# A gated-scan and Hadamard FFN layer: an earlier load of x, a norm's ScalarE work spread over two units, and transposes evicted by VectorE alone

## The chip, the cores and the metric

The kernel runs on one core of a Trainium2 chip. The metric is the device time of one execution in microseconds (us); with one core there is no slowest core to look for. The engines are called as in the profile: PE is TensorE (PEld its weight loads), ACT is ScalarE, DVE is VectorE, POOL is GpSimd, SP is SyncE, which here only issues DMAs.

## What is computed

Four sequences (B = 4) of T = 512 tokens with D = 512 features pass through one layer, all in float32. Cut to what matters:

```python
def attn(h):                                   # Wi, Wf, Wg, Wo: 512 x 512
    i, f, g = h @ Wi.T, h @ Wf.T, h @ Wg.T
    gate = sigmoid(f)
    v = silu(i) * (1.0 - gate)
    o = scan over tokens of  o_t = gate_t * o_(t-1) + v_t
    o = o * rsqrt(mean(o * o) + 1e-5) * gnorm_w * silu(g)
    return o @ Wo.T

def ffn(h):                                    # W1, W3: 2048 x 512, W2: 512 x 2048
    hidden = silu(h @ W1.T) * (h @ W3.T)
    return fwht(hidden) @ W2.T                 # Walsh-Hadamard transform over 2048

x = x + layernorm(attn(layernorm(x)))
x = x + layernorm(ffn(layernorm(x)))
```

## The kernel before, in words

**Products.** Every large product is done by a Strassen-Winograd scheme: seven products of quarter blocks instead of eight. `seven` (L387) makes the seven steps in the order P1, P2, P6, P5, P7, P3, P4 (`ORDER`, L31). P1, P6, P7 and P4 add up in one PSUM bank, called X; P5 and P3 in a bank Z; P2 has a bank Y. Each step is eight matmuls into its bank, and then the bank as it stands goes to a quarter of the result in SBUF: ACT copies it at P1, P6, P5 and P4 (L413), DVE adds it to what lies there at P2, P7 and P3 (L411). (Where the result is itself added to an older one, all seven are DVE additions.) Since P6 goes on adding into the bank of P1, it must wait until that bank was copied; in the same way P3 waits for the copy of P5, and P4 for the addition of P7.

**Units.** One call of `project` is a unit: two projections of 512 tokens by 128 or 256 features. A sequence has three attention units (`attn_unit`, L450) and eight FFN units m = 0 to 7 (`ffn_unit`, L533). In an FFN unit the result d_f is followed by ACT's Silu (L535), DVE's product ht (L441) and four DVE sums over blocks of ht (L122 to L125). Every two FFN units, `ffn_out` (L549) multiplies their ht with the transformed W2 (X_po, Y_po, Z_po at L559); the transform of W2 itself runs between the products as `transform_high` and `transform_low` (h and g).

**Order.** PE and SP run in the order in which the program calls them. Between two products of a unit, `run` (L99) calls `slot`, which takes the next waiting piece of other work from the list `fill` (down projections, transposes, W2's transform): after each product where the unit is dense, else after products 1, 3, 5 and 6. ACT, DVE and POOL are ordered by the framework's scheduler, by priorities (`high_priority`) and by `behind(what)` (L207), which lets a block be issued only after the instruction last noted under that name in `read`: "P7" is the latest DVE addition of a P7, "copy" the latest ACT copy of a bank.

**x and the norms.** x of a sequence is loaded by `load_x` (L112) as four tiles of 256 KB. `normalize_tiles` (L236) makes a layernorm of two of its four 128-token tiles: statistics and their root on DVE and POOL (L252, L253, L218, L221, L229), then one ACT instruction per tile that writes xn (L262). For the first sequences (`ON_TENSOR`, L234) PE transposes xn (`transposes`, L327): in two halves h = 0 and 1, each with one 128x256 piece of four PSUM banks, of which ACT copies two (L348) and DVE two (L350); after the second half DVE forms four sums of blocks (L129 to L132), which the products P6, P5, P7 and P4 read. For all other norms ACT writes xn in a permuted order, POOL issues its write to DRAM (xnd, L270), and `load_fold` (L358) reads it back through SP as fold, which DVE transposes in 32x32 blocks (L378) and sums up.

**The places concerned.** In FFN unit 3 of sequence 0, x of sequence 2 is loaded (L757). Ahead of FFN unit 4 of sequences 0 and 1 the attention norm of sequences 2 and 3 is made (L759), in one piece; in unit 6 its fold is loaded (L761), and in unit 7 it is transposed (L763).

Of the kernel before, what the change touches and what calls it, by code (L numbers as in the profile page):

```python
# [42 lines left out]
def kernel(  # L43
# [14 lines left out]
    nc = tc.nc  # L58
    B, T, D = x.shape
# [25 lines left out]
    def bank(name):  # L85
        return psum.tile([P, 2, H], F32, tag="ps", name=name)
# [4 lines left out]
    fill = deque()  # L91

    def slot():
        if fill:
            make = fill.popleft()
            if make is not None:
                make()

    def run(products, dense):  # L99
        for k, make in enumerate(products):  # L100
            make()
            if dense or k in (1, 3, 5, 6):
                slot()

# [7 lines left out]
    def load_x(b):  # L112
        xs[b] = xpool.tile([P, NT, D], F32, tag="x", name=f"x_{b}")
        for i in range(NT):
            eng = nc.scalar if b == 0 else nc.sync
            eng.dma_start(out=xs[b][:, i, :], in_=x[b, ts(i, P), :])
# [10 lines left out]
    def combine_right(t, eng):  # L127

        eng.tensor_sub(t[:, T1], t[:, B12], t[:, B11])  # L129
        eng.tensor_sub(t[:, T2], t[:, B22], t[:, T1])  # L130
        eng.tensor_sub(t[:, T3], t[:, B22], t[:, B12])
        eng.tensor_sub(t[:, T4], t[:, B21], t[:, T2])  # L132
# [33 lines left out]
    def combine_weights(n=None):  # L166
        for _ in range(len(uncombined) if n is None else n):
            key, t = uncombined.pop(0)
            combine_left(t, nc.vector)
            kept(key, t)  # L170
# [9 lines left out]
    def load_ffn_w(b, m):  # L180
        ffn_w[b, m] = weight(w1, "w1", m, b), weight(w3, "w3", m, b)
# [25 lines left out]
    def behind(what):  # L207


        return tc.issue_after(read[what].ins)  # L210
# [13 lines left out]
    def scales(mv, eps, name):  # L224

        n = mv.shape[1]
        r = inverse_root(mv, eps, name)
        nb = small.tile([P, n], F32, tag="nb", name=f"nb_{name}", bufs=4)
        i = nc.vector.scalar_tensor_tensor(nb, mv[:, :, 0], -1.0, r, ALU.mult, ALU.mult)  # L229
        return r, nb, i  # L230

    xns, xnd = {}, {}
# [3 lines left out]
    def normalize_tiles(b, name, i0, n, later=False):  # L236

        if (name, b) not in xns:
            xns[name, b] = work.tile(
                [P, NT, D], F32, tag="wide", name=f"xn_{name}_{b}", bufs=3
            )
        t = xns[name, b]
        st = small.tile([P, n, 6], F32, tag=f"st{n}", name=f"st_{name}_{b}_{i0}")
        mv = small.tile([P, n, 2], F32, tag=f"mv{n}", name=f"mv_{name}_{b}_{i0}")  # L250
        for k in range(n):
            nc.vector.bn_stats(st[:, k, :], xs[b][:, i0 + k, :])  # L252
            nc.vector.bn_aggr(mv[:, k, :], st[:, k, :])  # L253
        r, nb, read["nb"] = scales(mv, EPS, f"{name}_{b}_{i0}")

        def apply():
            for k in range(n):
                x_t, to = xs[b][:, i0 + k, :], t[:, i0 + k, :]
                if (name, b) not in ON_TENSOR:
                    x_t = x_t.rearrange("p (i a c) -> p i c a", c=ND, a=32)  # L260
                    to = to.rearrange("p (i c a) -> p i c a", c=ND, a=32)
                read["xn"] = nc.scalar.activation(  # L262
                    to, x_t, AF.Identity, bias=nb[:, k : k + 1], scale=r[:, k : k + 1]
                )
            if (name, b) not in ON_TENSOR:
                if (name, b) not in xnd:
                    xnd[name, b] = scratch.tile(
                        [NT, P, D], F32, tag=f"xn_{name}_{b}", name=f"xnd_{name}_{b}"
                    )
                nc.gpsimd.dma_start(  # L270
                    out=xnd[name, b][i0 : i0 + n].rearrange("t p d -> p t d"),
                    in_=t[:, i0 : i0 + n, :],
                )

        if later:
            return apply
        apply()

    def normalize(b, name, n=2):
        for i in range(0, NT, n):  # L280
            normalize_tiles(b, name, i, n)
# [45 lines left out]
    def transposes(b, name):  # L327

        xn = xns.pop((name, b))
        xt = work.tile([P, 7, 2, H], F32, tag="xt", name=f"xt_{name}_{b}", bufs=2)
        xts[name, b] = xt
        pt = []

        def make(h):
            if h == 0:
                pt.extend(bank(f"pt_{name}_{b}_{c}") for c in range(ND))  # L340
            for i in range(2 * h, 2 * h + 2):
                for c in range(ND):
                    nc.tensor.transpose(pt[c][:, h, ts(i % 2, P)], xn[:, i, c::ND], ident)
            with tc.high_priority(offset=URGENT):
                for c in range(ND):
                    to = xt[:, (B11, B12)[h] if c < 2 else (B21, B22)[h], c % 2, :]
                    if c % 2:
                        nc.scalar.copy(to, pt[c][:, h, :])  # L348
                    else:
                        read["xt"] = nc.vector.tensor_copy(to, pt[c][:, h, :])  # L350
                if h:
                    combine_right(xt, nc.vector)

        return [partial(make, h) for h in range(2)]
# [190 lines left out]
    def load_down_w(b, part):  # L545
        for m in range(part * NS, (part + 1) * NS):
            down_w[b, m] = again(("w2", m), b, stream2)
# [108 lines left out]
    def transform_low(m):  # L656

        def make(k):  # L660
            w = low_w[m]
            if k == 0 and m + 2 < NU:
                load_low(m + 2)
            blocks = ((B11, B12), (B21, B22))[k]
            t = w[:, blocks[0] : blocks[1] + 1 : blocks[1] - blocks[0]]
            p = bank(f"g_{m}_{k}")
            nc.tensor.matmul(p, h16_sb, t, start=True, stop=True)
            nc.scalar.mul(t, p, 1.0 / FF**0.5)
            if k == 1:
                combine_right(w, nc.vector)  # L670
                kept(("w2", m), w)

        return [partial(make, k) for k in range(2)]
# [33 lines left out]
    with behind("P3"):  # L707
        with tc.high_priority(offset=URGENT):
            combine_weights(2)
        with tc.high_priority(offset=SOON):  # L710
            apply = [normalize_tiles(1, "a", i, 2, True) for i in (0, 2)]
# [6 lines left out]
        with behind("P2"):  # L718
            prepare_wo(wo_t[0])

    def norm_behind_copy():
        with behind("copy"):
            for make in apply:
                make()

    fill.extend([wo_behind_sum, norm_behind_copy] + transposes(1, "a"))
    attn_unit(0, 2)
    load_attn_w(1, 1)
    fill.extend([None] * 3 + attn_out(0))
# [11 lines left out]
    for b in range(B):  # L741
        last = b == B - 1
        for m in range(NU):
            if m + 1 < NU:
                load_ffn_w(b, m + 1)
            if b == 0 and m % NS == 0:
                for k in range(m + 2, min(m + 2 + NS, NU)):
                    fill.extend(transform_low(k))
            if m == 0 and not last:
                fill.extend([None] * 4 * (b > 0) + attn_out(b + 1))  # L750
            if m and m % NS == 0:
                if last and m == NU - NS:
                    fill.extend([None] * 8)
                fill.extend([None] + ffn_out(b, m // NS - 1))
            if m % NS == 1:
                load_down_w(b, m // NS)
            if m == 3 and b == 0:  # L757
                load_x(2)
            if m == 4 and b + 2 < B:  # L759
                normalize(b + 2, "a")  # L760
            if m == 6 and not last:  # L761
                load_fold(*((b + 2, "a") if b + 2 < B else (b + 1, "f")))
            if m == NU - 1 and not last:  # L763
                transpose_fold(*((b + 2, "a") if b + 2 < B else (b + 1, "f")))
            ffn_unit(b, m, b == 0)
            with behind("P7"):
                combine_weights()
        tail = ffn_out(b, NU // NS - 1)
        if b + 2 < B:
            load_attn_w(b + 2, 0)  # L770
            load_fold(b + 1, "f")
            fill.extend([None] + tail)
            for u in range(3):
                if u < 2:
                    load_attn_w(b + 2, u + 1)
                else:
                    load_ffn_w(b + 1, 0)
                if u == 1:
                    transpose_fold(b + 1, "f")
                attn_unit(b + 2, u)  # L780
            if b + 3 < B:
                load_x(b + 3)
        elif not last:
            load_ffn_w(b + 1, 0)
            fill.extend([None] + tail)
        else:
            fill.extend(tail)
            flush()
# [34 lines left out]
```

## Time and profile before

| what | value |
|---|---|
| median of 3 runs | 840.94 us (840.87 to 841.08) |
| the profiled execution | 841.11 us |
| its span from first to last instruction | 839.3 us |
| mean granted PE clock | 0.993 |
| x of sequence 2: issued, landed | 195.44 to 197.7, 206.4 to 208.6 us |
| xn of sequence 2 on ACT (4 tiles) | 211.98 to 217.3 us |
| xn of sequence 3 on ACT (4 tiles) | 394.34 to 401.9 us |
| ACT instruction for one permuted tile of xn, mean | 1.28 to 1.35 us |
| ACT copy of one bank (128x512) | 0.58 us |
| DVE addition of one bank (128x512) | 0.69 us |
| PE, eight 128x256 matmuls of one product, start to start | 1.73 us |

The profile's page lists the busy time of each engine, the chain of work that ended last, groups of instructions by source line with the wait in front of them, and DMA transfers. A timeline gives each engine's instructions in order of time, with the number of equal instructions that were merged, and in brackets how long the engine stood before, and what ended that. A name such as X_f is the PSUM bank X of an FFN unit; X_a is one of an attention unit, X_po one of a down projection. "out<-in" are the tiles written and read. Only what stands in PE's way, or slows its clock, can be seen in the span directly.

### The profile page before, as it was taken

The page shows a single profiled execution, that of the slowest core. Times are in us where ns is not written, and L with a number is a line of the kernel's source. Part 1 is how long each engine was busy: PE and PEld are TensorE (multiplying, and loading weights), DVE is VectorE, ACT ScalarE, POOL GpSimd, SP SyncE. Part 2 cuts the span into 40 slices and gives each one's busy share as a digit, 9 for nine tenths or more (in the row PEclk, how much of TensorE's full clock was granted, in tenths as well). Part 3 has the DMA queues.
Part 4 walks back from the last instruction along what each step waited for, and adds up shares of the span by engine and source line. Part 5 has one row for each costly group of instructions (what it writes and reads, how often), then busy time and mean ns, then how long its engine had stood idle before and what let it go on. Part 6 is the DMA issues. An engine that isn't in the chain of part 4 may idle for free.

```text
span 839.3 us, 9824 instructions
## 1 busy us (share of the span) xinstructions
PE 817.5 (97%) x3728; PEld 703.8 (84%) x3728; DVE 457.6 (55%) x920; ACT 269.1 (32%) x386; POOL 68.9 (8%) x112
## 2 busy tenths in 40 slices
PE   7999999999799999999999999999999999999995
PEld 4788888888688888888888888888888888888884
DVE  6386796754656557537435545737336434534445
ACT  4554462532311225227312123524321121322111
POOL 5120101210200001003000000102000000100000
PEclk9999999999899999999999999999999999999998
DMA  9995369596968625826563622835353642625101
GB/s 335 414 409 211 110 230 348 210 343 239 330 209 263 231 88 184 355 89 254 182 197 156 202 88 95 330 152 197 117 214 90 273 174 89 226 94 214 70 19 50
DMA packets 65743, 169.54 MB, mean 202 GB/s; under 512 B 4768, under 2 KB 40224, under 8 KB 65696
## 3 DMA queue, kind: packets, MB, share of 16 engines
q1 hardware_dynamic: 56528, 125.65, 42.3%
q0 software_dynamic: 8448, 41.96, 12.7%
q10 hardware_dynamic: 720, 1.31, 0.4%
q8 instruction: 29, 0.48, 0.2%
q14 instruction: 18, 0.15, 0.0%
HBM read 125.90 MB, written 42.99 MB: 201 GB/s over the span
## 4 chain that ended last, share of the span: by engine, by line
PE 84%; DVE 5%; DMA 5%; ACT 2%; issue 2%; SPq 1%; POOL 1%; POOLq 0%; DVEq 0%; ACTq 0%
PE X_f L426 23%; PE X_po L559 12%; PE Z_f L426 12%; PE X_a L426 8%; PE Z_po L559 6%; PE Y_f L426 6%; PE Z_a L426 5%; PE Y_po L559 3%; PE X_y L512 3%; DMA w2p<-in_W_dram 3%; PE Y_a L426 2%; PE Z_y L512 2%; DMA x<-in_x_dram 2%; DVE x L316 1%; PE Y_y L512 1%
## 5 line engine op out<-in xcount | busy, mean ns | idle before, releaser
L426 PE MATMUL X_f<-xt_f,w 128*128 128x256 f32 x1024 | 241.5, 379 | 0.9 <-ACT d_f L413 0.9
L426 PEld LDWEIGHTS X_f<-xt_f,w 128*128 128x128 f32 x1024 | 194.1, 190 | 30.6 <-issue 2.9
L413 ACT COPY d_f<-X_f 128x512 f32<-128x512 f32 x96 | 56.0, 583 | 301.2 <-PE X_f L426 267.1
L426 PE MATMUL Z_f<-xt_f,w 128*128 128x256 f32 x512 | 122.9, 384 | 4.7 <-ACT d_f L413 4.7
L559 PE MATMUL X_po<-w,ht 128*128 128x256 f32 x512 | 121.7, 381 | 0.2 <-DVE f L411 0.2
L426 PEld LDWEIGHTS Z_f<-xt_f,w 128*128 128x128 f32 x512 | 98.2, 192 | 20.3 <-ACT d_f L413 5.5
L559 PEld LDWEIGHTS X_po<-w,ht 128*128 128x128 f32 x512 | 97.9, 191 | 14.1 <-DVE f L411 0.6
L411 DVE TENSOR_TENSOR f<-X_po,f 128x512 f32<-128x512 f32 x51 | 35.1, 688 | 97.1 <-PE X_po L559 97.0
L441 DVE TENSOR_TENSOR ht<-d_f 128x1024 f32<-128x1024 f32 x32 | 39.0, 1218 | 63.6 <-ACT d_f L535 49.9
L559 PE MATMUL Z_po<-w,ht 128*128 128x256 f32 x256 | 60.5, 379 | 0.0
L426 PE MATMUL Y_f<-xt_f,w 128*128 128x256 f32 x256 | 60.5, 379 | 0.0
L426 PEld LDWEIGHTS Y_f<-xt_f,w 128*128 128x128 f32 x256 | 48.6, 190 | 7.9 <-issue 0.7
L559 PEld LDWEIGHTS Z_po<-w,ht 128*128 128x128 f32 x256 | 48.6, 190 | 6.6
L221 POOL TENSOR_TENSOR rs_f<-rs_f,power 128x2 f32<-128x2 f32 x16 | 14.0, 878 | 428.7 <-DVE nm_f L308 406.8
L413 ACT COPY d_a<-X_a 128x512 f32<-128x512 f32 x36 | 21.0, 583 | 79.4 <-PE X_a L426 62.1
L411 DVE TENSOR_TENSOR d_f<-X_f,d_f 128x512 f32<-128x512 f32 x32 | 22.1, 689 | 33.0 <-PE X_f L426 31.8
L535 ACT ACTIVATE d_f<-d_f 128x1024 f32<-128x1024 f32 x32 | 33.8, 1055 | 0.9
L426 PE MATMUL X_a<-xt_a,wi 128*128 128x256 f32 x128 | 33.0, 380 | 0.8 <-DVE xt_a L130 0.8
L411 DVE TENSOR_TENSOR d_f<-Z_f,d_f 128x512 f32<-128x512 f32 x32 | 22.0, 687 | 21.0 <-PE Z_f L426 21.0
L426 PE MATMUL X_a<-xt_a,wf 128*128 128x256 f32 x128 | 32.9, 379 | 0.0
L411 DVE TENSOR_TENSOR f<-Z_po,f 128x512 f32<-128x512 f32 x28 | 19.2, 684 | 24.9 <-PE Z_po L559 24.9
L426 PEld LDWEIGHTS X_a<-xt_a,wi 128*128 128x128 f32 x128 | 24.1, 190 | 8.5 <-issue 4.2
(154 smaller groups left out, 1005.6 us busy)
## 6 DMA issues: line engine op xcount, KB each, us to landing
w<-s_w SPq DMA_DIRECT2D x80, 896.0 KB, 6.4
s_w<-w POOLq DMA_DIRECT2D x24, 896.0 KB, 5.9
w<-in_W_dram SPq DMA_DIRECT2D x32, 256.0 KB, 6.0
wi<-s_wi SPq DMA_DIRECT2D x6, 896.0 KB, 10.8
wf<-s_wf SPq DMA_DIRECT2D x6, 896.0 KB, 6.9
wg<-s_wg SPq DMA_DIRECT2D x6, 896.0 KB, 5.3
wo<-s_wo SPq DMA_DIRECT2D x6, 896.0 KB, 9.2
w_h<-w2p POOLq DMA_DIRECT2D x8, 512.0 KB, 8.5
```

The source lines that it names most:

```text
L221: read["power"] = nc.gpsimd.tensor_tensor(r, r, power_t[:, 0:n], ALU.pow)
L316: nc.vector.scalar_tensor_tensor(x_t, self.y[:, i, t, :], r[:, t : t + 1], x_t, ALU.mult, ALU.add)
L411: read[what] = nc.vector.tensor_add(to, ps[which], to)
L413: read["copy"] = nc.scalar.copy(to, ps[which])
L426: nc.tensor.matmul(ps[:, n, :], w[:, a, c, :], xt[:, bb, c, :], start=first and n == 0 and c == 0, stop=c == 1, skip_group_check=True,)
L441: nc.vector.tensor_mul(to.rearrange("p (t k) f -> p k t f", t=2), a.rearrange("p k (t f) -> p k t f", t=2), b2.rearrange("p k (t f) -> p k ...
L512: nc.tensor.matmul(ps[:, t, :], og[:, a, c, ts(t, P)], w[c][:, bb, :], start=first and t == 0 and c == 0, stop=c == 1, skip_group_check=True,)
L535: nc.scalar.activation(d[:, 0], d[:, 0], AF.Silu)
L559: nc.tensor.matmul(ps[:, t, :], hts[b, m][:, a, ts(t, P)], w[m][:, bb, :], start=first and t == 0 and m == ms[0], stop=m == ms[-1], skip_g ...
```

## The change

Three things are changed.

- x of sequence 2 is loaded in FFN unit 2 instead of unit 3, ahead of the next pieces of W2 in SP's order.
- The attention norms of sequences 2 and 3: their statistics are issued behind the latest DVE addition of a P7, and their ACT instructions one tile at a time, each behind the latest ACT copy of a bank. The first two come after products 3 and 5 of unit 4 (P5 and P3), the other two after products 0 and 3 of unit 5 (P1 and P5); `run` finds them in the new dictionary `beside`. The write to DRAM follows when the second tile of a pair is made. `norm_behind_copy` becomes the more general `behind_copy`.
- In the second half of PE's transposes DVE copies all four pieces. That concerns three norms: the attention norms of sequences 0 and 1, and the FFN norm of sequence 0.

```diff
+    beside = {}
+
     def run(products, dense):
         for k, make in enumerate(products):
             make()
+            for other in beside.pop(k, ()):
+                other()
             if dense or k in (1, 3, 5, 6):
                 slot()
...
-        def apply():
-            for k in range(n):
+        def apply(tiles=range(n)):
+            for k in tiles:
                 x_t, to = xs[b][:, i0 + k, :], t[:, i0 + k, :]
...
-                nc.gpsimd.dma_start(
-                    out=xnd[name, b][i0 : i0 + n].rearrange("t p d -> p t d"),
-                    in_=t[:, i0 : i0 + n, :],
-                )
+                if tiles[-1] == n - 1:
+                    nc.gpsimd.dma_start(
+                        out=xnd[name, b][i0 : i0 + n].rearrange("t p d -> p t d"),
+                        in_=t[:, i0 : i0 + n, :],
+                    )
...
-                    if c % 2:
+                    if c % 2 and h == 0:
                         nc.scalar.copy(to, pt[c][:, h, :])
                     else:
                         read["xt"] = nc.vector.tensor_copy(to, pt[c][:, h, :])
...
-    def norm_behind_copy():
+    def behind_copy(*makes):
         with behind("copy"):
-            for make in apply:
+            for make in makes:
                 make()
 
-    fill.extend([wo_behind_sum, norm_behind_copy] + transposes(1, "a"))
+    fill.extend([wo_behind_sum, partial(behind_copy, *apply)] + transposes(1, "a"))
...
-            if m == 3 and b == 0:
+            if m == 2 and b == 0:
                 load_x(2)
             if m == 4 and b + 2 < B:
-                normalize(b + 2, "a")
+                with behind("P7"):
+                    late = [normalize_tiles(b + 2, "a", i, 2, True) for i in (0, 2)]
+            if m in (4, 5) and b + 2 < B:
+                for t, k in enumerate((3, 5) if m == 4 else (0, 3)):
+                    beside[k] = [partial(behind_copy, partial(late[m - 4], range(t, t + 1)))]
```

## The prediction

> **What bounds the kernel now.** I read the busy shares first, then TensorE's waits, then the chain and the timeline around its longest waits. The shares say one engine is the bound:
>
> ```profile
> PE 817.5 (97%) x3728; PEld 703.8 (84%) x3728; DVE 457.6 (55%) x920; ACT 269.1 (32%) x386; POOL 68.9 (8%) x112
> ```
>
> An edit that only rearranges other engines can gain no more than what PE stands still or runs slow. TensorE's waits (engine, line, what it waited for; us, times, longest), without those for the first load:
>
> ```profile
> PE Z_f L426 <- ACT d_f L413: 4.7, 2, 4.5
> PE X_f L426 <- ACT d_f L413: 0.9, 2, 0.7
> PE X_a L426 <- DVE xt_a L130: 0.8, 1, 0.8
> ```
>
> The first two are a product that accumulates into a PSUM bank which ACT has not copied out yet. The 4.5 us in PE's timeline (start, us, instructions, idle before):
>
> ```profile
> 206.03 1.89 PE L426 MATMUL Z_f<-xt_f,w 128*128 128x256 f32 x8
> 207.76 1.02 PE L667 MATMUL g<-w,had 128*128 128x512 f32 x2
> 208.62 1.89 PE L426 MATMUL X_f<-xt_f,w 128*128 128x256 f32 x8
> 214.98 3.78 PE L426 MATMUL Z_f<-xt_f,w 128*128 128x256 f32 x8 [4.47 <-ACT d_f L413]
> 218.56 2.70 PE L559 MATMUL X_po<-w,ht 128*128 128x256 f32 x8
> 221.10 1.89 PE L426 MATMUL X_f<-xt_f,w 128*128 128x256 f32 x8
> ```
>
> Eight such matmuls take 1.73 us start to start. And why ACT is late, in the chain and in the whole timeline:
>
> ```profile
> 195.91 12.70 DMA x<-in_x_dram
> ...
> 211.78 0.17 DVE nb_a L229
> ```
> ```profile
> 195.44 2.22 SPq L116 DMA_DIRECT2D x<-in_x_dram  x4
> ...
> 206.23 0.60 ACT L668 ACTIVATE w<-g 128x512 f32<-128x512 f32 x1 [0.27 <-DMA x<-in_x_dram]
> ...
> 211.98 2.48 ACT L262 ACTIVATE xn_a<-x,nb_a,rs_a 128x512 f32<-128x512 f32 x2 [5.15 <-DVE nb_a L229]
> ...
> 214.37 0.56 ACT L413 COPY d_f<-Z_f 128x512 f32<-128x512 f32 x1
> ```
>
> x of sequence 2 is issued at 195.44 and lands at 208.6; ACT stands 5.15 us in front of a norm whose statistics hang on it; the copy of Z_f, whose product was done at 207.9, is queued behind two norms. The same thing, smaller, with sequence 3, whose x was there long before:
>
> ```profile
> 400.55 1.33 ACT L262 ACTIVATE xn_a<-x,nb_a,rs_a 128x512 f32<-128x512 f32 x1
> 401.77 0.57 ACT L413 COPY d_f<-X_f 128x512 f32<-128x512 f32 x1
> ```
>
> **What the Trainium skill says.** "TensorE: Matmul & The Clock Gate", section "What's actually happening": after an idle window of about 3.4 us the array falls back to half its clock. The trace agrees: after the 4.47 us gap eight matmuls span 3.78 instead of 1.89 us, and the window 209 to 221 has a granted clock of 0.72. After gaps below 1 us they span 1.99. "Perfetto Trace Analysis", "Sequencer Loop": an engine's instruction waits in its queue for its semaphore; ACT's copy above shows what that costs the one behind it. "DMA: Bandwidth & Descriptors", "Issuing engines are not separate DMA queues": all transfers share the same 16 engines, so moving x moves its load, too. Here x took 10.9 to 12.7 us at a DMA share of 0.96 (window 195 to 209), while weight loads at 155 us took 6.5 to 7.1.
>
> **The change part by part**, from the order of instructions in both kernels. PE's order does not change; what follows is on PE's old clock.
>
> 1. *x of sequence 2 sooner.* SP now issues its four 256 KB pieces behind unit 3's weights (last one at 158.2, 0.69 us), so from 158.9. SP's next item, w2_h pieces, was issued at 177.18 after a wait, so nothing on SP is delayed unless x's issue itself takes 18 us. The last two pieces wait for the w2 loads issued at 154.43, which took 4.5 and 6.4 us. With 12.7 us to land, x is there by 175. It lands in a full stretch (DMA share 0.98 from 158 to 168, 0.87 to 178, 1.05 to 188); 1 MB at 350 GB/s is 3 us, and 188 to 195 is at 0.05. Those displaced have room: unit 3's weights landed near 165 and are first read at 172.64 by DVE. Cost 0; if that cover were gone, up to 3 us.
>
> 2. *Statistics behind P7.* DVE's four bn_stats (0.58 each), four bn_aggr and two adds, some 2.8 us, go in front of ht_3's product, which waited 2.74 us for ACT's Silu until 200.19. They start when w_4's sums end, 196.66, so ht_3 starts near 200.3. Cost 0.1, and nothing on PE waits for ht_3 before 212.
>
> 3. *xn spread.* In unit 4 ACT's order becomes: Z_f copy, xn, eviction of w_7's second half, xn, copy of P4; tiles 2 and 3 go behind the first and third copy of unit 5. The Z_f copy is then done at 208.55, and P3 may start at 210.35 (208.62 + 1.73). Old start of the first undisturbed product: 221.10; new: 210.35 + 2 x 1.73 = 213.81: **7.29 us gained**, 4.63 of it the gap and 2.66 the slow clock behind it. Next in line is P4 at 213.8. It needs DVE's addition of P7, now behind w_7's three combinations, which wait for the eviction behind xn: 208.55 + 1.22 + 0.6 = 210.4, three at 0.34, the addition 0.69: 212.1. 1.7 us of room. In unit 5 ACT was idle 6.32 and 8.05 us before its copies, enough for 1.28 each.
>
> 4. *The second write of xnd_a* leaves POOL behind unit 5's Z_f copy (236.84 + 0.58) and xn (1.28), so at 238.8 and lands, with 4.1 us for such writes, at 243.6 after its issue of 0.73. SP reaches fold_a at 246.60 because a weight load ahead of it waits for PE. 3.0 us of room, cost 0. For sequence 3: issue at 425.4, landed 430.2, fold_a at 431.68.
>
> 5. *Sequence 3's norm* (unit 4 of sequence 1). The two xn pairs leave the stretch from 394 to 402; the copy of X_f, whose product ended at 398.1, no longer waits. PE's timeline has Z_po at 399.84, the late X_f at 402.40 and the next at 404.23; undisturbed, that one would start at 399.84 + 2 x 1.73 = 403.30. **0.93 gained.** PE's other small waits on ACT (170.55, 532.43) have nothing to do with the edit and stay.
>
> 6. *Transposes' second half on DVE.* Two copies more, 0.34 each, three times; two ACT copies less. In sequence 1 (62 us) the order on DVE also changes: one og product of 1.13 now stands behind the sums. Old: L130, which PE waited for, started at 65.42. New: copies from 61.64 to 62.98, L129 0.6, one og 1.13, L130 at 64.71, ending at 65.39. PE starts 0.14 later at 65.53 instead of 66.25: **0.72 gained.** In sequence 0 (16 us) the order turns against it: the addition of Y_a now stands ahead of L130. Copies 15.99 to 17.33, L129 to 18.0, Y_a's product ends at 18.05, addition from 18.15, L130 18.75 to 19.43, PE at 19.56 instead of 18.74: **0.82 lost**, and 0.07 for a first matmul group after a gap (1.10 against 1.03 at 66.25). The bounds: 0 if the addition starts at once, 1.6 if the two copies' 0.68 come on top. I take 0.89. It isn't absorbed at 35.45, where PE waited for ACT's eviction, which moves along. For the FFN of sequence 0 (115 us) L130 ended at 118.2 and is read at 122.70: 0.7 later costs nothing.
>
> Sum: -7.29 - 0.93 - 0.72 + 0.89 = -8.05 us. On the profiled span that is 839.3 to 831.25; that execution took 841.11, 1.8 more than its span and 0.2 more than the median of 840.94, so 840.94 - 8.05 = 832.9 us.
>
> **Rivals.**
> - *A smaller stall takes its place.* DVE's addition of P7 in unit 4 (point 3) has 1.7 us of room, and unit 4's DVE queue is packed: DVE was busy 12.39 of 24.3 us there, now within 16.9. If evictions or combinations come 3 to 6 us later, PE stands 1.3 to 4.3 us: 834.2 to 837.2. For it: an in-order queue with three kinds of waits. Against: each duration is from the trace.
> - *The early eviction costs more and sequence 1 gains nothing*: +1.6 at 18 us, 0 at 66: -6.6, 834.3. Against: both orders are static and nothing else waits there.
> - *Slower: fold_a waits for the late second write.* SP stands at fold_a, behind it w2_6, w2_7, wi and wf. Beyond 3.0 us of room each us delays the fold, which landed at 257.9 and was transposed by DVE from 260.31, 2.4 later; after that DVE stands at the transposes, with the additions of the running products queued behind them. I give those 3 us before PE notices (an estimate, a little under two products of 1.73). So PE stands from 3.0 + 2.4 + 3 = 8.4 us of lateness on, and the kernel is slower than before beyond 8.4 + 8.05 = 16.5 us: with 20 us, 844.4. For it: half the tensor leaves some 20 us later than before (217.62). Against: such writes took 4.1 us.
> - *The change doesn't do what it says*: x issued earlier but held by its queue. Pieces three and four do wait for earlier loads, but those landed by 161.3.
>
> **How the numbers follow.** Forecast 0.78, its own range 831.5 to 834.5 (early cost 0 to 1.6, the 66 us gain 0 to 1). Smaller stall 0.11, early eviction 0.06, slower 0.04; no difference (something unseen eats it) 0.01. 831.0 to 836.8 leaves out the tail of the first rival, the slower case, and little below. A measurement of this kernel can tell about 0.2%, 1.7 us; so faster 0.95, same 0.01, slower 0.04.
>
> **What would show it.** PE's wait at unit 4 gone, no matmul group of 3.78 us, granted clock 1.0 there; x landed before 178; ht_3's product still waiting for Silu; ACT's copy of Z_f within 0.2 us of its product; PE's wait on L130 near 66 us shrunk to 0.3, and a new one of 0.8 near 19 us on L130. Wrong if PE waits for DVE's addition in unit 4, or if SP waits at fold_a.

## The result and the profile after

The changed kernel takes 833.51 us, the median of four executions (833.40 to 834.04), against 841.01 us for the kernel before (840.87 to 842.14). The ratio is 0.9909, with a 95% interval of 0.9892 to 0.9926. The forecast was 832.9 with a range of 831.0 to 836.8. The profiled execution's span went from 839.3 to 831.6 us.

Busy shares of the changed kernel, from the page:

```profile
PE 814.6 (98%) x3728; PEld 702.2 (84%) x3728; DVE 459.8 (55%) x926; ACT 267.9 (32%) x380; POOL 69.2 (8%) x112
```

TensorE has the same 3728 matmuls and is busy 2.9 us less: that is the clock, not work. Its waits (engine, line, what it waited for; us, times, longest):

```profile
PE h L643 <- DMA w2p<-in_W_dram: 5.3, 1, 5.3
PE X_a L431 <- ACT w2p L644: 0.7, 1, 0.7
PE X_f L431 <- ACT d_f L418: 0.3, 1, 0.3
PE X_f L431 <- DVE w L127: 0.2, 1, 0.2
PE Z_f L431 <- ACT d_f L418: 0.2, 1, 0.2
```

Of the 4.7 us of Z_f behind ACT's copy 0.2 are left, and the 0.8 us on the sum of xt_a are gone from the list. Two waits are new: 0.7 us at X_a and 0.2 us on a weight's sum, on L127. The view puts the first down to ACT's copy of h, but in the kernel before the same product started at 18.74 us, ahead of the end of that copy (19.53), so it doesn't need it. It reads a sum of xt_a from DVE's queue (L134 here is L130 of the kernel before):

```profile
19.01 0.68 DVE L134 TENSOR_TENSOR xt_a<-xt_a 128x512 f32<-128x512 f32 x1
```

The product starts at 19.84 us, 0.15 after the end of this sum. That is the wait on L130 near 19 us that the prediction named. Unit 4 in TensorE's timeline of the changed kernel (start, us, instructions), at the place where the 4.47 us gap was:

```profile
206.59 1.89 PE L431 MATMUL Z_f<-xt_f,w 128*128 128x256 f32 x8
208.31 1.02 PE L672 MATMUL g<-w,had 128*128 128x512 f32 x2
209.17 1.89 PE L431 MATMUL X_f<-xt_f,w 128*128 128x256 f32 x8
210.90 1.89 PE L431 MATMUL Z_f<-xt_f,w 128*128 128x256 f32 x8
212.63 1.89 PE L564 MATMUL X_po<-w,ht 128*128 128x256 f32 x8
214.35 1.89 PE L431 MATMUL X_f<-xt_f,w 128*128 128x256 f32 x8
```

The second Z_f follows the X_f without a gap, and no group takes 3.78 or 2.70 us any more. ACT's timeline beside it:

```profile
208.51 0.59 ACT L418 COPY d_f<-Z_f 128x512 f32<-128x512 f32 x1 [1.13 <-PE Z_f L431]
209.00 1.31 ACT L266 ACTIVATE xn_a<-x,nb_a,rs_a 128x512 f32<-128x512 f32 x1
210.21 0.58 ACT L673 ACTIVATE w<-g 128x512 f32<-128x512 f32 x1
210.69 1.32 ACT L266 ACTIVATE xn_a<-x,nb_a,rs_a 128x512 f32<-128x512 f32 x1
```

The copy waits for TensorE's Z_f and for nothing else, and the norms stand behind it, one at a time. The window from 209 to 221 us now has a granted clock of 1.00 (third figure from the end):

```profile
209.00:221.00 12.00, 12.00 (x56) 10.43 (x55) 8.55 (x20) 5.92 (x8) 2.35 (x4) 1.00 1.03 364
```

To find where the rest of the time went, I laid the start of every TensorE group after beside that before, and noted where the distance jumps. Where TensorE waits for a load that lands at its own time, what was lost or gained ahead of that place no longer counts; this is called eaten below.

| place in the kernel before | jump, us | what it is |
|---|---|---|
| 5 to 15 us | +0.24 | first load of W2 landed 0.33 later, part of it made good |
| 18.74 us, X_a of sequence 0 | +0.93 | transposes' second half on DVE |
| 35.45 us, h | -0.23 | eaten by a wait for a load |
| 58 to 66 us, transposes and X_a of sequence 1 | -0.89 | transposes' second half on DVE |
| 124 us, X_f of the first FFN unit | +0.50 | transposes' second half on DVE |
| 206 to 221 us, unit 4 of sequence 0 | -7.30 | the stall and its slow clock |
| 402 us, unit 4 of sequence 1 | -0.94 | sequence 3's norms |
| sum | -7.69 | spans: -7.7 |

### The profile page after: what moved, and what is told of

Read it like the earlier page. It is cut to its first block, busy times and chain, and to the rows that moved or that the text cites. A ratio compares the mean times of both kernels' runs of the same rounds, so it can differ in the third digit from the quotient of the medians.

```text
span 831.6 us, 9833 instructions
## 1 busy us (share of the span) xinstructions
PE 814.6 (98%) x3728; PEld 702.2 (84%) x3728; DVE 459.8 (55%) x926; ACT 267.9 (32%) x380; POOL 69.2 (8%) x112
## 4 chain that ended last, share of the span: by engine, by line
PE 93%; DVE 4%; ACT 1%; issue 1%; DMA 0%; POOL 0%; POOLq 0%; DVEq 0%; SPq 0%; ACTq 0%
PE X_f L431 25%; PE Z_f L431 13%; PE X_po L564 13%; PE X_a L431 10%; PE Z_po L564 7%; PE Y_f L431 6%; PE Z_a L431 5%; PE X_y L517 3%; PE Y_po L564 3%; PE Y_a L431 3%; PE h L643 2%; PE Z_y L517 2%; PE g L672 1%; PE Y_y L517 1%; DVE x L321 1%
## 5 line engine op out<-in xcount | busy, mean ns | idle before, releaser
L431 PE MATMUL Z_f<-xt_f,w 128*128 128x256 f32 x512 | 121.1, 379 | 0.2 <-ACT d_f L418 0.2
```

Source lines behind the costliest of these rows:

```text
L431: nc.tensor.matmul(ps[:, n, :], w[:, a, c, :], xt[:, bb, c, :], start=first and n == 0 and c == 0, stop=c == 1, skip_group_check=True,)
```

## The experiments

All are built from the kernel before or the changed one. Medians are of four or more executions. The ratio is to the kernel before, run beside it on the same chip (medians of before: 841.83 for the first four runs, 842.09 for the next four, 841.76 for the last four). Each of these three groups ran on a chip of its own, so a small difference between medians of two groups shows little.

| variant | median, us (range) | ratio (95% interval) |
|---|---|---|
| before, x sooner only | 834.90 (834.10 to 835.72) | 0.9922 (0.9907 to 0.9937) |
| changed, without x sooner and without the transposes' edit | 835.38 (834.97 to 835.88) | 0.9928 (0.9912 to 0.9945) |
| before, transposes' edit only | 841.87 (841.57 to 842.91) | 1.0001 (0.9993 to 1.001) |
| changed, without the transposes' edit | 833.63 (833.52 to 834.40) | 0.9909 (0.9894 to 0.9924) |
| changed, transposes' edit in sequence 1 only | 832.53 (832.32 to 833.16) | 0.9888 (0.9874 to 0.9903) |
| changed, last W2 pieces ahead of x | 833.73 (833.29 to 834.06) | 0.9900 (0.9884 to 0.9917) |
| the same, without the transposes' edit | 832.86 (832.75 to 833.24) | 0.9892 (0.9877 to 0.9907) |
| the same, transposes' edit in sequence 1 only | 832.38 (831.87 to 832.47) | 0.9884 (0.9869 to 0.9899) |
| changed, fold_a a unit later | 837.91 (836.69 to 840.98) | 0.9957 (0.9942 to 0.9972) |
| the same, second pair of norms a unit later | 838.66 (837.31 to 839.41) | 0.9960 (0.9947 to 0.9972) |
| changed, again | 833.55 (833.31 to 838.86) | 0.9912 (0.9894 to 0.9930) |
| W2 ahead and edit in sequence 1 only, again | 832.13 (832.00 to 833.17) | 0.9888 (0.9874 to 0.9902) |

### What removes the stall: the load, or the order on ACT?

The prediction put the 7.29 us down to the spread norms and called the load free. Each alone shows whether that is right. First the load alone, in the kernel before:

```diff
-            if m == 3 and b == 0:
+            if m == 2 and b == 0:
                 load_x(2)
```

> The kernel before with one edit: x of sequence 2 is loaded a unit sooner (m == 2). The norm's instructions keep their urgency and stand ahead of bank copies; with x there sooner, ACT's queue has the four norms in unit 3 instead of unit 4. Theory A (the stall of unit 4 came from the late x alone): no product waits for ACT's copy of Z_f at 206 us, -7.3 us, and the norms of unit 3 cost what those of sequence 3 cost, 0 to 1.2: 833.7 to 834.9. Theory B (copies have to go ahead of the norms): the four norms of 1.28 each in unit 3 hold back a copy there and a stall of 2 us or more with its slow matmuls stays: 836 to 839.

It took 834.90 us; its trace shows -7.29 us at unit 4 and nothing at sequence 3. The scheduler builds ACT's order anew for this kernel, so the norms also stand elsewhere. ACT's timeline in unit 3, where they are now:

```profile
183.18 1.31 ACT L262 ACTIVATE xn_a<-x,nb_a,rs_a 128x512 f32<-128x512 f32 x1 [1.60 <-DVE nb_a L229]
184.39 0.56 ACT L413 COPY f<-X_po 128x512 f32<-128x512 f32 x1
184.85 3.70 ACT L262 ACTIVATE xn_a<-x,nb_a,rs_a 128x512 f32<-128x512 f32 x3
188.46 0.56 ACT L413 COPY f<-Z_po 128x512 f32<-128x512 f32 x1
188.93 0.58 ACT L413 COPY d_f<-X_f 128x512 f32<-128x512 f32 x1
```

Three norms stand in front of two copies for 3.70 us, and TensorE runs through. Z_f's copy in unit 4 then has nothing ahead of it (same kernel, same view):

```profile
209.47 0.58 ACT L413 COPY d_f<-Z_f 128x512 f32<-128x512 f32 x1 [1.13 <-PE Z_f L426]
```

So the stall came from norms that waited for x. Norms whose x is there cost nothing here, and 0.94 us at sequence 3, where an urgent copy stands behind one. Theory A holds; its allowance of up to 1.2 us for unit 3 was not needed. That the median still lies at its upper end is not explained by unit 3: the profiled execution is 1.5 us later than the kernel before by 67 us, 0.7 of it in the first 15 us and 0.8 at a product h that waited 0.96 us for a load (below).

Then the spread norms and their statistics alone, with x as late as before (the edit is against the changed kernel):

```diff
-            if m == 2 and b == 0:
+            if m == 3 and b == 0:
                 load_x(2)
...
-                    if c % 2 and h == 0:
+                    if c % 2:
```

> The changed kernel without the earlier load (x of sequence 2 still issued near 195 us) and without the edit of the transposes: only the statistics behind P7 and the spread of the norms. Theory A (without x in time the wait moves from ACT to DVE): four statistics stand on DVE before x lands at 208.6, behind them w_6's and w_7's combinations and P7's addition, which PE needs at 213.8; 2.3 us of statistics and 2 us of combinations later that is 213 to 216, a stall of 0 to 3 us: -5 to -8.2, 833 to 836. Theory B (order of ACT's queue is all): PE doesn't stand in unit 4 and the gain is 7.3 + 0.93 = 8.2: 832.8. Theory C (the early x is what counts): only 0.93 of sequence 3 is gained: 840.

It took 835.38 us, within theory A's 833 to 836. In its trace unit 4 gains 5.4 us net and sequence 3 0.94. DVE's timeline of this kernel:

```profile
207.00 0.69 DVE L256 BATCH_NORM_STATS2 st_a<-x 128x6 f32<-128x512 f32 x1 [2.57 <-DMA x<-in_x_dram]
209.20 0.69 DVE L256 BATCH_NORM_STATS2 st_a<-x 128x6 f32<-128x512 f32 x1 [1.50 <-DMA x<-in_x_dram]
...
212.35 0.16 DVE L233 SCALAR_TENSOR_TENSOR nb_a<-mv_a,rs_a 128x2 f32<-128x2 f32 x1 [0.61 <-POOL rs_a L225]
...
215.45 0.68 DVE L416 TENSOR_TENSOR d_f<-X_f,d_f 128x512 f32<-128x512 f32 x1
```

and TensorE's:

```profile
212.69 1.89 PE L564 MATMUL X_po<-w,ht 128*128 128x256 f32 x8
216.19 2.00 PE L431 MATMUL X_f<-xt_f,w 128*128 128x256 f32 x8 [1.60 <-DVE d_f L416]
```

The statistics stand 2.57 and 1.50 us for x, the combinations of w_6 and w_7 behind them, and P7's addition starts at 215.45 instead of 211.84 in the changed kernel, so TensorE stands 1.60 us. DVE waited for x in the kernel before, too (2.56 and 1.57 us), but there ACT's late copy ended later and hid it; with the copy ahead of the norms, DVE's is the wait that ends last. The Trainium skill, "Perfetto Trace Analysis", section "Sequencer Loop", says that an engine's instruction is pushed into the engine's queue and waits there for its semaphores; that those behind it wait, too, is what this timeline shows. It is also the mechanism of the first rival ("a smaller stall takes its place"), which needed a late x to become real.

The two edits overlap: 7.29 and 5.4 + 0.94 us alone, 8.24 together. The stall needed both, a late x and a copy queued behind the norms that wait for it, and each edit takes away one of the two. The load alone brings all of unit 4; what the spread adds to it is 0.94 us at sequence 3. The trace of the changed kernel without the transposes' edit differs from the load alone by just that: -0.84 and -0.10 us at 396 us, nothing else after 37 us.

### What the transposes' edit costs, and where

Alone in the kernel before:

```diff
-                    if c % 2:
+                    if c % 2 and h == 0:
                         nc.scalar.copy(to, pt[c][:, h, :])
```

> The kernel before with one edit: the second half of PE's transposes goes out by DVE alone. Theory (the terms read from the two traces, on TensorE's start times): +0.93 at 19 us, -0.23 at 36, -0.18 at 60, -0.71 at 66, +0.50 at 124: +0.3 us, 841.3. Rival (the edit is a gain, since ACT has two copies less each time): 840.2 or less. Second rival (the two copies' 0.68 us come on top at 19 us): 842.

Measured: 841.87 us, no difference that can be told from zero. The interval, 0.6 us below to 0.8 above, holds the theory's +0.3 and leaves out the rival's gain of 0.8 and the second rival's loss of 1. More than that it can't tell, and the trace tells why: the +0.93 us at 19 us is there, but h, at 37.56 us, waited 0.57 us for a piece of W2 that landed late in this execution. That landing set its start, so the loss before it was eaten in this execution.

The changed kernel with this edit taken back:

> The changed kernel with the transposes evicted as before (half by ACT). Theory: unit 4 and sequence 3's norm keep their -7.3 and -0.94, and the edit's +0.3 goes: 832.7 to 833.2, no slower than the changed kernel. Rival (DVE alone is needed, because the spread norms on ACT get in the way of the copies): slower than the changed kernel, 834 or more.

It took 833.63 us, above the 832.7 to 833.2 that I expected and level with the changed kernel. TensorE's timeline of its profiled execution (834.40 us, the slowest of the four):

```profile
37.00 1.10 PE L643 MATMUL h<-w2p,had 128*128 128x512 f32 x2 [1.26 <-DMA w2p<-in_W_dram]
```

The 0.93 us won at 19 us turned into a wait of 1.26 us for the load. The same product before the change:

```profile
35.45 1.10 PE L638 MATMUL h<-w2p,had 128*128 128x512 f32 x2 [0.18 <-DMA w2p<-in_W_dram]
```

There the prediction took the wait for one on ACT that moves along; the line says it is a load. The piece leaves SP at 17.8 us, behind x of sequence 1, and lands 17 to 20 us after its issue. To take this cover away, four kernels followed. The first moves the edit, the second the load, and the other two join them:

```diff
-                    if c % 2 and h == 0:
+                    if c % 2 and (h == 0 or (name, b) != ("a", 1)):
```

> The changed kernel, with DVE evicting the second half alone only in the norm of sequence 1 (the transposes at 62 us); the other two as before. Theory (the edit's terms lie at different places and can be had one by one): the wait of 1.0 us on L134 near 67 us shrinks to 0.3, no wait on L134 near 19 us, no wait for w_3's sum near 124 us: 0.7 us less than the kernel with all transposes as before (833.6), so 832.9. Rival (what is gained at 67 us is taken by the next product): 833.6.

```diff
-    load_x(1)
     load_w2(range(6, NJ))
+    load_x(1)
```

> The changed kernel, with the last two w2 pieces loaded ahead of sequence 1's x instead of behind it. In five traces the product h at 36 us starts when such a piece lands (waits of 0.18 to 1.26 us, none in two), so what is lost or gained before 36 us is eaten there. Theory (absorption): with the piece there sooner h doesn't wait, its start is set by PE alone, and the 0.9 us that the edit of the transposes costs at 19 us stays: 0 to 0.3 us below the changed kernel. Rival (the piece lands as late as before, since the transfers share their engines): no difference.

> The changed kernel with the transposes as before and the last two w2 pieces loaded ahead of sequence 1's x. Theory (absorption): the wait of 1.26 us at 37 us goes: 1.0 to 1.3 us below the same kernel with the pieces behind x, 832.4, and 0.3 (0.93 - 0.18 - 0.71 + 0.50, less what the first waits differ) to 0.5 below the changed kernel with the pieces ahead. Rival (h starts when the transfers allow it): equal to it.

> The changed kernel with the edit of the transposes in sequence 1 alone and the last two w2 pieces ahead of sequence 1's x: no wait at 19, 36 and 124 us, a wait of 0.3 at 66. Theory: the sum of both gains, 0.7 below the kernel with all transposes as before and the pieces ahead, 1.3 to 2 below the changed kernel: 831.7. Rival (x of sequence 1 comes too late for its norm): a wait at the transposes near 58 us and no gain.

With the pieces ahead of x no execution profiled waits at 36 us any more (TensorE, pieces ahead, transposes as before):

```profile
34.85 1.03 PE L431 MATMUL Y_a<-xt_a,wf 128*128 128x256 f32 x4
35.72 1.02 PE L643 MATMUL h<-w2p,had 128*128 128x512 f32 x2
```

For the changed kernel this brings nothing (833.73 against 833.51 and 833.55), since in its two profiled executions h came late anyway and didn't wait; the theory's 0 to 0.3 us and the rival's zero cannot be told apart there. Without the transposes' edit it brings 0.8 us (832.86 against 833.63), less than the 1.0 to 1.3 that I expected; these two ran on different chips. Between the two kernels with the pieces ahead, which ran on one chip, nothing is eaten, and the edit costs 0.87 us of median. Their traces show the terms one by one: +0.93 at 19 us, -0.89 at 66, +0.49 at 124, together +0.53, and 0.2 from the start of the run. Used in sequence 1 alone it keeps the -0.89 and nothing else behind the first 15 us; of the medians 0.48 is seen (832.38 against 832.86; the two ranges do not meet). In the kernel with the pieces behind x it gives 832.53, against 833.63 on the other chip, more than the 0.7 I expected; in its profiled execution h did not wait. On one chip the kernels with this edit differ by 0.15 us with the pieces ahead of x or behind it, and their ranges overlap, so no gain of the moved load is shown there.

The +0.50 at 124 us is the term that the prediction did not have. It is in every trace with the edit in all three norms, and in none with it in sequence 1 alone. DVE's timeline before (og is the attention's gated output, w a block of a weight):

```profile
119.44 2.36 DVE L441 TENSOR_TENSOR og<-o,d_a 128x1024 f32<-128x1024 f32 x2
121.72 0.42 DVE L123 TENSOR_TENSOR w<-w 128x256 f32<-128x256 f32 x1
122.05 0.68 DVE L122 TENSOR_TENSOR og<-og 128x512 f32<-128x512 f32 x1
```

and in the changed kernel, with TensorE's two half groups below:

```profile
120.06 2.36 DVE L446 TENSOR_TENSOR og<-o,d_a 128x1024 f32<-128x1024 f32 x2
122.33 0.69 DVE L416 TENSOR_TENSOR d_f<-Y_f,d_f 128x512 f32<-128x512 f32 x1
122.93 0.69 DVE L126 TENSOR_TENSOR og<-og 128x512 f32<-128x512 f32 x1
123.53 0.42 DVE L127 TENSOR_TENSOR w<-w 128x256 f32<-128x256 f32 x1
```
```profile
122.76 1.03 PE L431 MATMUL X_f<-xt_f,w 128*128 128x256 f32 x4
124.01 1.13 PE L431 MATMUL X_f<-xt_f,w 128*128 128x256 f32 x4 [0.23 <-DVE w L127]
```

The 0.6 us of two more copies is not what hurts: the sum of w, 0.6 later than 122.14, would still end ahead of the second half of X_f. It is the order: a sum of the weight w that stood right behind og's products stands behind Y_f's addition and a sum of og as well, and ends 1.8 us later. TensorE needed it after half of X_f.

### What a late fold costs

The prediction's slower rival said that TensorE stands once the second write of xnd_a is 8.4 us late. Two kernels make fold_a and that write late. Both also load the fold at a later place of the program, and the scheduler then builds DVE's order anew, so they don't test the 8.4 us in the order of the changed kernel; no run does.

```diff
-            if m == 6 and not last:
+            if m == (7 if b + 2 < B else 6) and not last:
                 load_fold(*((b + 2, "a") if b + 2 < B else (b + 1, "f")))
```

> The changed kernel with fold_a of sequences 2 and 3 loaded a unit later (m == 7): it leaves SP behind the weights of the next unit, near 259 instead of 239.9, and lands near 271.5 instead of 252.5. A measure of what lateness of the fold costs. Theory A (as in the prediction: PE stands from 5.4 us of the fold's lateness on): 19 us late, so 13.6 us for each of two sequences, 27 in all: 861. Theory B (DVE's transposes are ordered behind other work, and PE reads xt_a first at 274.8): transposes and sums of some 5 us from 271.5 make 276.5, a stall of 1 to 3 us for each sequence: 836 to 840.

and, on top of it:

```diff
-            if m in (4, 5) and b + 2 < B:
+            if m in (4, 6) and b + 2 < B:
...
-                    beside[k] = [partial(behind_copy, partial(late[m - 4], range(t, t + 1)))]
+                    beside[k] = [partial(behind_copy, partial(late[m // 2 - 2], range(t, t + 1)))]
```

> The kernel with the late fold, and the second two norms of sequences 2 and 3 a unit later (unit 6), so that the second write of xnd_a leaves POOL near 256.5 instead of 232.2 and lands near 260.6, behind the place where SP reaches the fold. Theory (each us that the write lands behind SP's turn is added to the fold, and PE has no room left there): 0 to 2 us for each sequence above the kernel with the late fold. Rival (the fold has room before PE reads it): equal to it.

The first took 837.91 us and the second 838.66, 4.4 and 5.1 above the changed kernel on that chip; their ranges overlap, so by time they can't be told apart. The first is within theory B's range; theory A's 861 is far off. But theory B had the place wrong. For sequence 2 neither kernel makes TensorE stand, although in the second POOL's write leaves at 252.47 instead of 232.19 us and SP's fold at 255.62 instead of 239.88 (1.3 us of both differences is the later start of this execution). DVE's timeline of the second kernel, and TensorE's first reader of xt_a:

```profile
268.34 2.48 DVE L383 STREAM_TRANSPOSE xt_a<-fold_a 128x512 f32<-128x512 f32 x4
...
273.52 0.68 DVE L136 TENSOR_TENSOR xt_a<-xt_a 128x512 f32<-128x512 f32 x1
```
```profile
274.37 1.89 PE L431 MATMUL X_f<-xt_f,w 128*128 128x256 f32 x8
276.09 1.03 PE L431 MATMUL X_a<-xt_a,wi 128*128 128x256 f32 x4
```

Here a write 19 us later costs nothing: DVE's queue was built with the transposes some 14 us further back, and xt_a is ready 1.9 us before it is read. Apart from 1.4 and 1.3 us in the first 40 us of the two profiled executions, all of the loss is at sequence 3, in both kernels. For the kernel with the late fold, TensorE and DVE:

```profile
461.86 1.89 PE L564 MATMUL X_po<-w,ht 128*128 128x256 f32 x8
466.64 2.04 PE L431 MATMUL X_a<-xt_a,wi 128*128 128x256 f32 x4 [2.90 <-issue]
468.48 1.91 PE L431 MATMUL X_a<-xt_a,wf 128*128 128x256 f32 x4
470.19 1.91 PE L431 MATMUL Y_a<-xt_a,wi 128*128 128x256 f32 x4
471.89 1.46 PE L431 MATMUL Y_a<-xt_a,wf 128*128 128x256 f32 x4
```
```profile
463.76 1.23 DVE L446 TENSOR_TENSOR ht<-d_f 128x1024 f32<-128x1024 f32 x1 [2.74 <-ACT d_f L540]
464.90 0.69 DVE L416 TENSOR_TENSOR f<-X_po,f 128x512 f32<-128x512 f32 x1
465.50 0.42 DVE L126 TENSOR_TENSOR ht<-ht 128x256 f32<-128x256 f32 x1
465.83 2.48 DVE L383 STREAM_TRANSPOSE xt_a<-fold_a 128x512 f32<-128x512 f32 x4
```

The view names no cause for the 2.90 us; TensorE starts 0.14 us after the end of the first of the four transposes. They follow ht's sum back to back, and ht's product waited for ACT. The fold left SP 21.7 us later than in the changed kernel, but its last piece had landed by 460.7 us, 5 us before the first transpose. So it was the transposes' place in DVE's queue that set their start. TensorE stood 2.90 us and lost another 3.1 at a slow clock. This execution (840.98 us) is the slowest of its kernel; its 6.1 us at this place are more than the 4.4 of the medians.

The last two runs put the changed kernel and the best one side by side on one chip:

> The changed kernel once more, for a comparison on one chip: 833.5.

> The changed kernel with the edit of the transposes in sequence 1 alone and the last two w2 pieces ahead of sequence 1's x, once more, beside the changed kernel on one chip: 1.2 below it (832.3).

The better one is 1.4 us below (832.13 against 833.55). Its eight executions in two runs lie between 831.87 and 833.17, the ten of the changed kernel from 833.31 upward (nine up to 834.19, one at 838.86). So it beats both kernels, by 0.17% over the changed one. It is the changed kernel with two edits: DVE evicts alone only in sequence 1, and the last W2 pieces are loaded ahead of x; the first is the one whose gain is shown. The trace has neither of the two new waits.

## Why the prediction was right, and where it was not

The forecast was 0.6 us too low, and the sum by its own steps is -8.05 against -7.69 in the traces. That the sum is so close owes something to luck: a loss of 0.50 us that it lacked is in part offset by gains of 0.23 and 0.17 that it lacked, too (step 6).

1. *x sooner.* Right: the last piece was issued by 163.8 us and took at most 8.6, so x was there by 172.4, and SP's next item came at 178.08. But the credit is wrong. The step is costed at nothing and the gain is booked under step 3; the load alone brings the 7.29 us, the spread alone 5.4.
2. *Statistics.* Right: ht_3's product started at 200.75, right behind ACT's Silu (which ended at 200.71), no later than before on TensorE's clock.
3. *xn spread.* The number is right, -7.30 against -7.29, both parts: 4.63 for the gap, 2.67 for the clock. P7's addition ended at 212.52 and P4 started at 214.35, 1.8 us of room against 1.7. Given the early load the spread was not needed for it.
4. *Second write.* Right: it left at 232.19 (238.8 on the old clock, less the 6.8 us gained by then) and SP took the fold at 239.88 without a wait. The point from which lateness decides, 8.4 us, stays untested. It takes DVE's order as fixed; where the fold moves in the program that order is built anew, and in such a kernel 19 us cost sequence 2 nothing.
5. *Sequence 3's norm.* Right: -0.94 against -0.93, and the experiment with the load alone lacks just this.
6. *Transposes.* +0.93 against the predicted 0.89 at 19 us and -0.71 against -0.72 at 66 are right. With the transposes' start included the second is -0.89. The wait left near 66 us is 0.28 us (from start to start, beyond the usual 0.87), against 0.3. Two sentences failed. "For the FFN of sequence 0 (115 us) L130 ended at 118.2 and is read at 122.70: 0.7 later costs nothing" is true of that sum, but the step looked at that sum alone; a neighbour changed its place in DVE's order and cost 0.50. And "It isn't absorbed at 35.45, where PE waited for ACT's eviction, which moves along": the wait there is for a load, and 0.23 us was absorbed in this trace. In the list of waits that load has two for h, and the prediction set both aside as the first load's.

So the edit of the transposes, predicted to cost 0.17 us in sum (0.89 - 0.72), costs 0.53 by the traces and 0.87 by the medians with the load out of the way. Of what is left between forecast and measurement, 0.24 us is a later first load, and the medians of one kernel differ by up to 1 us between chips (841.01 to 842.09 for the kernel before).

## What to carry to other kernels

Ask of a stall what the order of a queue and the late arrival at its head each have to do with it, and try each alone: here an earlier load cured all of it, while the reordering without the load brought 5.4 of 7.3 us and laid bare the next engine's wait for the same x. When an edit adds work to an engine, compare the whole order of that engine around the place, not only the instruction that is read next. A wait for a load early in a kernel eats small gains and losses in front of it, so measure those with the load out of the way.

## What the runs showed of the hardware

A gap of 2.90 us was enough to slow TensorE's clock (kernel with the late fold): after it the groups of four matmuls took 2.04, 1.91, 1.91 and 1.46 us instead of 1.03, and from 466 to 473 us the granted clock was 0.52. From the start of the group before to the start behind the gap there are 3.05 us more than the usual 1.73. In the kernel with the later norms, after the same 2.90 us, they took 2.05 and 1.70 and then 1.03, at a granted clock of 0.76, so the price was 3.1 us once and 1.6 the other time; why they differ is not shown. The Trainium skill, "TensorE: Matmul & The Clock Gate", section "What's actually happening", gives about 3.4 us of idling for this and says that the window runs freely; here less was enough, and the measurement decides. After 1.60 us the next group of eight took 2.00 instead of 1.89 us, and after 1.26 us a pair of 128x512 matmuls 1.10 instead of 1.02.
